# A running maximum in the softmax over nodes: the context of the first 20 tiles is made at the end of the layer ahead

## The chip, the cores and the metric

The kernel runs on one core of a Trainium2 chip. A core has a matrix engine (TensorE, PE in the profile; its weight loads are shown apart as PEld), a vector engine (VectorE, DVE), a scalar engine for activation functions (ScalarE, ACT), GpSimd (POOL), a queue engine (SyncE, SP) and 16 DMA engines. Each engine takes its own instructions in a fixed order, and waits on semaphores for the others. Data lies in on-chip memory of 128 partitions; PE writes to PSUM, a small memory of eight banks. The metric is the time of one execution on the device in microseconds (us), the median of several runs.

## The reference

The reference is a graph network on 3125 nodes of 256 features. Its first part adds a convolution over 100,000 edges to a mixer of four layers; after it come a gated mixture of experts, a second graph convolution with another mixer, and a routed mixture of experts. The change is in the four layers of the first mixer:

```python
def _linear_attn(x, Wq, Wk, Wv, Wo, bo):
    b, n, dm = x.shape
    split = lambda t: t.reshape(b, n, HEADS, DH).transpose(0, 2, 1, 3)
    scale = DH ** (-0.25)
    q = jax.nn.softmax(split(x @ Wq) * scale, axis=-1)
    k = jax.nn.softmax(split(x @ Wk) * scale, axis=-2)
    v = split(x @ Wv)
    context = jnp.einsum('bhnd,bhne->bhde', k, v)
    out = jnp.einsum('bhnd,bhde->bhne', q, context)
    out = out.transpose(0, 2, 1, 3).reshape(b, n, dm)
    return out @ Wo + bo

def _forward(x, ...):
    for i in range(DEPTH):
        h = _layernorm(x, ln1_g[i], ln1_b[i])
        x = x + _linear_attn(h, Wq[i], Wk[i], Wv[i], Wo[i], bo[i])
        h = _layernorm(x, ln2_g[i], ln2_b[i])
        x = x + (jax.nn.gelu(h @ W1[i] + b1[i], approximate=False) @ W2[i] + b2[i])
    return x
```

There are 8 heads of 32 columns. The softmax of `q` runs over the 32 columns of a head, that of `k` over all 3125 nodes: every column of `k` needs its maximum over the nodes before the first exponential, and the sum of the exponentials divides the context.

## The kernel before

**Tiles and groups.** The nodes lie in 25 tiles of 128 rows (the last has 53). Four tiles make a group; groups 0 to 5 have four tiles, group 6 only the last, short tile. `xs` holds the state, `H` the normalized rows with a column of ones, `K` and `Q` the keys and queries of all tiles, all in on-chip memory.

**One layer.** A layer starts when the keys and queries of all tiles are there. `kmax` (L960, L962) holds for each partition the maximum over the tiles so far. The layer transposes it (L987), reduces it over the partitions (L988) and brings it back as a row on all partitions by transposing a broadcast (L991). Then for each group DVE subtracts the maximum from `K` (L995), and ACT takes the exponential (L996); after these, ACT takes the exponentials of `Q` (L999). `shares(g)` (L1007 to L1009) divides the queries of a group by their sums. `context(b)` (two blocks of 128 columns) multiplies the exponentials of `K` with `H` over all 25 tiles (L1030) into one PSUM bank; the column of ones gives the sum. A float32 matmul of the program is two passes in the profile, so the 50 matmuls of a layer are 100 instances of L1030. The mean is scaled by the reciprocal sum (L1034, L1035), transposed (L1039), scaled and shifted (L1041), multiplied with the value weights (L1046), masked to heads (L1048), and multiplied with the output weights (L1051); `cw` (L1053) is what `attended(g)` multiplies the queries with (L1074), before it adds to `xs` (L1076).

**The rest of the layer** goes over the groups: for group g, the attention of group g+2, the norms of group g+2 and of group g-1, the MLP's hidden rows (`experts_hidden`, L284 and L287, Gelu on ACT) and its second half (`forward`, L1093, the bias row L839, the addition L1098). While group g is in its MLP, group g-1 already makes its keys and queries of the next layer (`keyed_queries`, L951 to L962). So at the end of a layer the MLP of the short group 6 runs, then the norm of group 5 (L194 and L195 for the statistics, L168 to L173 for a reciprocal root by Newton steps, L205, and on ACT L211, which writes `H`), its transposes (L230, L232), its key matmuls (L951), and those of group 6. In the first layer the keys come straight from the input, in a loop of its own.

**Work beside it.** Two generators are woven in between the matmuls: the building of the adjacency matrix (`g_` names, L718 to L731) and the sorting of the gating edges (`b_` names: matmuls L489, L491 and L506, DVE work L471 to L522, DMAs that fetch `kr` and `b_to`, and GpSimd's scatter L431). They are taken in turns counted per matmul group, not in time.

**Order.** The program's order is given by the generators and the calls to `next`, but a scheduler places the instructions on the engines, and so decides what stands ahead of what on each engine. Buffers are pools: the tag `mm` (two PSUM banks) serves the key matmuls, the hidden rows and the context; `hid` (eight buffers) serves the hidden rows, and at the start of a layer the means.

Of the kernel before, what the change touches and what calls it, by code (L numbers as in the profile page):

```python
# [8 lines left out]
F32 = mybir.dt.float32  # L9
BF16 = mybir.dt.bfloat16  # L10
I32 = mybir.dt.int32
AF = mybir.ActivationFunctionType
OP = mybir.AluOpType
AX = mybir.AxisListType
# [3 lines left out]
P = 128  # L18
N = 3125
D = 256  # L20
# [36 lines left out]
AT_FIRST = 0.4  # L57
OF_GATING = 1.28
LAG = 8
OF_SPLIT = 0.5  # L60
BETWEEN = 0.6
ALONE = 1.25
# [10 lines left out]
def rows_of(t):  # L73
    return P if t < NT - 1 else LAST


def tiles_of(g):
    return list(range(4 * g, min(4 * g + 4, NT)))
# [25 lines left out]
def tile_gps(ctx: ExitStack, tc: tile.TileContext, a, out):  # L104
# [691 lines left out]
    with ExitStack() as st:  # L796
# [120 lines left out]
        def begin(g):  # L917

            r, x, k = rows_of(tiles_of(g)[-1]), rows_in(K, g), len(tiles_of(g))
            rstd, nmr = ln_stats(x, r, twice=True)  # L920
            scaled(rows_in(H, g), x, r, rstd, nmr, k)
            scaled(rows_in(xs, g), x, r, rstd, nmr)
            store_rows(xn_d, xs[:, tiles_of(g)[0]:tiles_of(g)[-1] + 1, :], g)
# [10 lines left out]
        def turned(g, l, ln):  # L934
            nx = rows_in(H, g)
            hT = mp.tile([P, 2, 512], F32, name="hT", tag="hT", bufs=2)
            transposed(ps, hT, nx, rows_of(tiles_of(g)[-1]), [fcol(f"{ln}_g", 2 * l + c) for c in range(2)],
                       [fcol(f"{ln}_b", 2 * l + c) for c in range(2)])
            return hT

        def meanwhile(g):

            return min(1, len(tiles_of(g)) - 1)

        def keyed_queries(l, g, hT, j, wqkv, kmax):

            t = tiles_of(g)[j]
            r = rows_of(t)
            pqk = ps.tile([P, 512], F32, name="mm", tag="mm", bufs=2)
            for k in range(2):  # L950
                pace[0] = T.matmul(pqk[:r], lhsT=hT[:, k, j * P:j * P + r], rhs=wqkv[:, k, 0:512],  # L951
                                   start=(k == 0), stop=(k == 1))
            qmax = small.tile([P, 8], F32, name="qmax", tag="qmax")
            q3 = pqk[:r, 0:D].rearrange("p (h d) -> p h d", d=32)
            V.tensor_reduce(qmax[:r], q3, axis=AX.X, op=OP.max)
            V.tensor_tensor(Q[:r, t, :].rearrange("p (h d) -> p h d", d=32), q3,
                            qmax[:r, :, None].to_broadcast([r, 8, 32]), op=OP.subtract)
            S.activation(K[:r, t, :], pqk[:r, D:2 * D], AF.Copy)
            if t == 0:
                V.tensor_copy(kmax, pqk[:, D:2 * D])  # L960
            else:
                V.tensor_tensor(kmax[:r], kmax[:r], pqk[:r, D:2 * D], op=OP.max)  # L962

        def most():
            return mp.tile([P, D], F32, name="kmax", tag="kmax")

        wqkv, kmax = weights[0], most()
        begin(0)
        hT = turned(0, 0, "ln1")
        for g in range(NG):  # L970
            this = hT
            if g + 1 < NG:
                begin(g + 1)
            for j in range(len(tiles_of(g))):
                keyed_queries(0, g, this, j, wqkv, kmax)
                if g + 1 < NG and j == meanwhile(g):
                    hT = turned(g + 1, 0, "ln1")
                next(first, None)

        for l in range(LAYERS):  # L980
            last = l == LAYERS - 1
            wo, w1, w2 = weights[-3:]
            graph.summed()
            pt = ps.tile([P, 512], F32, name="tr", tag="tr", bufs=2)
            kmT = small.tile([P, 2], F32, name="kmT", tag="kmT")
            for c in range(2):
                T.transpose(pt[:, c * P:(c + 1) * P], kmax[:, c * P:(c + 1) * P], ident)  # L987
            V.tensor_reduce(kmT, pt[:, :D].rearrange("p (c n) -> p c n", c=2), axis=AX.X, op=OP.max)  # L988
            pb = ps.tile([P, 512], F32, name="tr", tag="tr", bufs=2)
            for c in range(2):  # L990
                T.transpose(pb[:, c * P:(c + 1) * P], kmT[:, c:c + 1].to_broadcast([P, P]), ident)  # L991
            some = [(tiles_of(g)[0], tiles_of(g)[-1] + 1, rows_of(tiles_of(g)[-1])) for g in range(NG)]
            for t0, t1, r in some:
                kg = K[:r, t0:t1, :]
                V.tensor_tensor(kg, kg, pb[:r, None, :D].to_broadcast([r, t1 - t0, D]), op=OP.subtract)  # L995
                S.activation(kg, kg, AF.Exp, scale=scale)  # L996
            for t0, t1, r in some:
                qg = Q[:r, t0:t1, :]
                tc.keep_in_program_order(S.activation(qg, qg, AF.Exp, scale=scale))  # L999
# [24 lines left out]

            def context(b):

                pc = ps.tile([P, 512], F32, name="mm", tag="mm", bufs=2)
                for t in range(NT):
                    r = rows_of(t)
                    T.matmul(pc[:, :D + 1], lhsT=K[:r, t, b * P:(b + 1) * P], rhs=H[:r, t, :],  # L1030
                             start=(t == 0), stop=(t == NT - 1))
                    if t % 6 == 5:
                        yield
                V.reciprocal(ksum[:, b:b + 1], pc[:, D:D + 1])  # L1034
                S.activation(mean[:, b, :], pc[:, :D], AF.Identity, scale=ksum[:, b:b + 1])  # L1035
                yield
                pt = ps.tile([P, 512], F32, name="tr", tag="tr", bufs=2)
                for c in range(2):
                    T.transpose(pt[:, c * P:(c + 1) * P], mean[:, b, c * P:(c + 1) * P], ident)  # L1039
                for c in range(2):  # L1040
                    S.activation(meanT[:, b, c, :], pt[:, c * P:(c + 1) * P], AF.Identity,  # L1041
                                 scale=fcol("ln1_g", 2 * l + c), bias=fcol("ln1_b", 2 * l + c))
                yield
                po = ps.tile([P, D], F32, name="o", tag="o", bufs=2)
                for c in range(2):
                    T.matmul(po[:, :P], lhsT=wqkv[:, c, 512 + b * P:512 + (b + 1) * P], rhs=meanT[:, b, c, :],  # L1046
                             start=(c == 0), stop=(c == 1))
                V.tensor_tensor(ctxT[:, b, :], po[:, :P], mask32, op=OP.mult)  # L1048
                yield
                po = ps.tile([P, D], F32, name="o", tag="o", bufs=2)  # L1050
                T.matmul(po, lhsT=ctxT[:, b, :], rhs=wo[:, b, :], start=True, stop=False)  # L1051
                add_row(po, l, P, 0, eighth)
                S.activation(cw[:, b, :], po, AF.Copy)  # L1053
                yield

            two = [context(0), context(1)]
            for _ in range(5):
                next(two[0])
            for _ in range(4):
                next(two[1])  # L1060
                next(two[0], None)
            next(two[1])
            qT = queries(0)
            for _ in two[1]:
                graph.summed()
# [39 lines left out]
            for g in range(NG):  # L1105
                n, k = cols_of(g), len(tiles_of(g))
                again = g - 1 if g and not last else None
                if g + 2 < NG:
                    attended(g + 2)
                normal(*([g + 2] if g + 2 < NG else []), *([] if again is None else [again]))  # L1110
                if g + 4 < NG:
                    shares(g + 4)
                hid = experts_hidden(ps, mp, w1, hT, n, 8, [fcol("mix_b1", 8 * l + i) for i in range(8)], bufs=8,
                                     between=hidden if k == 4 else None)
                before = None if again is None else turned(again, l + 1, "ln1")
                for j in range(max(k, 4 if before else 0)):
                    if j < k:
                        forward(g, hid, j)
                        if k == 4 or last:
                            beside(share)  # L1120
                            spread(0.5 * share)
                    if k < 4 and j == 0 and not last:
                        normal(g)
                    if g + 1 < NG and j == meanwhile(g):
                        hT = turned(g + 1, l, "ln2")
                    if before:
                        keyed_queries(l + 1, again, before, j, wqkv, kmax)
                        if k == 4:
                            beside(BETWEEN)
                            spread(BETWEEN)  # L1130
            if not last:
                before = turned(NG - 1, l + 1, "ln1")
                keyed_queries(l + 1, NG - 1, before, 0, wqkv, kmax)
                weights = [out_weights(l + 1), *hidden_weights(l + 1)]
        for _ in gating:
            buckets.scattered()
# [1100 lines left out]
```

## Time and profile before

| | |
|---|---|
| median of 3 runs | 3774.78 us (3763.15 to 3776.9) |
| the profiled execution: its time | 3769.39 us |
| its span | 3767.6 us |
| mean granted clock of PE in it | 0.959 |
| starts of the four layers, first L1030 | 93.0, 444.2, 853.9, 1243.2 us |
| first L1074 of the layers | 124.1, 475.7, 885.4, 1274.5 us |
| L1030, all layers | 400 passes, 103.9 us busy, 9.6 us idle ahead |
| L995 (DVE) and L996 (ACT), all layers | 28 each, 28.8 and 26.6 us busy |

The mixer takes about the first 1,600 us of the span. PE, DVE and ACT are named with the line of the kernel that issued the instruction; a row of the profile in order of time gives the start, the length, the engine, the line, the operation, what it writes and reads, the shape and the number of instructions put together, and in brackets the idle time before them with what ended it.

### The profile page before, as it was taken

How to read it: one execution, taken by the hardware profiler on the slowest of the kernel's cores; microseconds unless marked ns; L12 is line 12 of the kernel's file. 1: busy time of each engine (PE TensorE's matmuls, PEld its weight loads, DVE VectorE, ACT ScalarE, POOL GpSimd, SP SyncE). 2: the span in 40 equal slices, each digit the busy share in tenths (PEclk: the TensorE clock that was granted, in tenths of full speed). 3: DMA queues.
4: the chain of work that ended last, by engine and by line, in shares of the span. 5: the costliest groups of instructions: out<-in, count | busy, mean ns of one | idle time of the engine just before them, and what ended most of it. 6: DMA issues, size and time to landing. Idle time of an engine off the chain costs nothing. (4 is left out here: it accounts for less than half of the span.)

```text
span 3767.6 us, 50246 instructions
## 1 busy us (share of the span) xinstructions
PE 3492.3 (93%) x18153; PEld 2118.1 (56%) x18153; DVE 1903.1 (51%) x6827; ACT 1119.7 (30%) x2092; POOL 910.7 (24%) x915
## 2 busy tenths in 40 slices
PE   7999989988999988899899999998999999999998
PEld 3656666556666656544465565554444444444687
DVE  8757757676677766200418888762013032223421
ACT  5333342334332433200236675330013000000233
POOL 0044234532454154300002322200014010000233
PEclk9999999999999999999899999999999999999999
DMA  7013424651446166542476662003211222221576
GB/s 212 20 37 45 60 42 49 60 71 30 53 59 73 24 90 84 108 133 68 134 231 169 165 184 82 15 12 125 83 50 47 67 70 62 60 61 50 152 184 148
DMA packets 347700, 326.90 MB, mean 87 GB/s; under 512 B 144052, under 2 KB 311757, under 8 KB 346011
## 3 DMA queue, kind: packets, MB, share of 16 engines
q1 hardware_dynamic: 212763, 280.87, 28.2%
q10 hardware_dynamic: 105424, 26.40, 7.7%
q0 software_dynamic: 29232, 16.09, 2.7%
q8 instruction: 151, 2.47, 0.3%
q14 instruction: 130, 1.06, 0.1%
HBM read 239.75 MB, written 90.83 MB: 88 GB/s over the span
## 5 line engine op out<-in xcount | busy, mean ns | idle before, releaser
L431 POOL DMA_INDIRECT btab<-b_word,b_key x512 | 530.0, 1035 | 777.7 <-PE mm L284 408.2
L1190 PE MATMUL ag<-chb,xb 128*128 128x512 bf16 (+2 forms) x1950 | 404.1, 367 | 24.5 <-DMA chb<-A 16.6
L1190 PE MATMUL ag<-chb,Hb 128*128 128x512 bf16 (+1 forms) x1800 | 416.9, 385 | 3.9 <-issue 3.9
L284 PE MATMUL mm<-hT,w 128*128 128x512 f32 (+1 forms) x896 | 389.4, 571 | 8.0 <-DVE kmax L962 5.0
L1093 PE MATMUL o<-w,hid 128*128 128x256 f32 (+1 forms) x1600 | 388.7, 390 | 0.0
L1093 PEld LDWEIGHTS o<-w,hid 128*128 128x128 f32 (+1 forms) x1600 | 293.1, 191 | 51.1 <-issue 10.4
L1190 PEld LDWEIGHTS <-xb 128*128 128x128 bf16 (+1 forms) x2100 | 184.3, 98 | 243.4 <-issue 35.5
L1190 PEld LDWEIGHTS <-Hb 128*128 128x128 bf16 (+1 forms) x2100 | 183.9, 99 | 215.7 <-issue 22.0
L287 ACT ACTIVATE hid<-mm,fm 128x512 f32<-128x512 f32 (+1 forms) x336 | 210.7, 630 | 312.7 <-PE mm L284 281.4
L284 PEld LDWEIGHTS mm<-hT,w 128*128 128x128 f32 x896 | 162.1, 200 | 146.2 <-issue 128.1
L1392 PE MATMUL o<-f0w,hid 128*128 128x256 f32 (+1 forms) x800 | 216.3, 399 | 2.5 <-ACT hid L287 2.5
L951 PE MATMUL mm<-wqkv,hT 128*128 128x512 f32 (+1 forms) x400 | 207.3, 643 | 6.1 <-DVE kmax L962 3.4
L284 PE MATMUL mm<-xnT,f0w 128*128 128x512 f32 (+1 forms) x448 | 204.8, 582 | 5.3 <-DVEq L1656 4.1
L475 DVE SCALAR_TENSOR_TENSOR b_junk<-kr,b_key,b_tri 128x128 bf16<-128x128 f32 x512 | 175.1, 342 | 27.3 <-DMA kr<-keys_g 24.0
L1783 POOL DMA_INDIRECT slots<-rb,r_ati x50 | 49.4, 987 | 501.3 <-DVE rb L1776 395.7
L731 ACT ACTIVATE g_st<-gc 128x400 bf16<-128x400 f32 x192 | 94.2, 500 | 255.4 <-PE gc L727 177.3
L1392 PEld LDWEIGHTS o<-f0w,hid 128*128 128x128 f32 (+1 forms) x800 | 141.5, 191 | 39.5 <-issue 14.7
L718 DVE TENSOR_TENSOR g_ol<-g_all,g_lo 128x1024 bf16<-128x1024 bf16 (+1 forms) x199 | 136.1, 684 | 40.9 <-PE gc L727 27.3
L2119 DVE TENSOR_TENSOR a2T<-a2T,ag 128x512 f32<-128x512 f32 x24 | 15.9, 688 | 277.4 <-PE ag L1190 277.3
L727 PEld LDWEIGHTS <-g_ol 128*128 128x128 bf16 (+1 forms) x1589 | 120.0, 165 | 61.4 <-issue 46.8
L232 ACT ACTIVATE hT<-tr,fm 128x512 f32<-128x512 f32 (+1 forms) x126 | 86.5, 719 | 164.1 <-PE tr L230 158.2
L1910 POOL DMA_INDIRECT out_dram<-yo,dest x56 | 87.5, 1562 | 189.8 <-DVE yo L1909 101.8
(504 smaller groups left out, 5697.5 us busy)
## 6 DMA issues: line engine op xcount, KB each, us to landing
hot<-low_d SPq DMA_DIRECT2D x125, 384.0 KB
kr<-keys_g SPq DMA_DIRECT2D x256, 128.0 KB
f1w<-in_f_w_dram SPq DMA_DIRECT2D x56, 512.0 KB
slots<-blank SPq DMA_DIRECT2D x14, 1950.0 KB
A<-g_st ACTq DMA_DIRECT2D x24, 800.0 KB
chb<-A SPq DMA_DIRECT2D x48, 397.2 KB
chb<-A SPq DMA_DIRECT2D x48, 384.0 KB
chb<-A SPq DMA_DIRECT2D x120, 128.0 KB
```

Of the source, the lines that this page charges most:

```text
L284: pace[0] = T.matmul(ph[:, :n], lhsT=w1[:, k, hb * P:(hb + 1) * P], rhs=xT[:, k, :n], start=(k == 0), stop=(k == 1))
L287: S.activation(h[:, :n], ph[:, :n], AF.Gelu, bias=bias[hb])
L431: d = G.indirect_dma_start(out=btab.rearrange("(n o) -> n o", o=1), out_offset=bass.IndirectOffsetOnAxis(ap=self.key[:, c:c + 1].bitcast(I ...
L475: ranked = V.scalar_tensor_tensor(junk, kr[:, (j % EACH) * P:(j % EACH + 1) * P], self.key[:, c0 + j:c0 + j + 1], self.tri, op0=OP.is_equa ...
L718: V.tensor_tensor(lo[:r, :, :k], self.all[:r, :, :k], self.lo[:r, None, c:c + k].to_broadcast([r, P, k]), op=OP.is_equal)
L727: T.matmul(p[:, j, :], lhsT=lo[:r, :, j], rhs=hi[:r, j, :h], start=True, stop=True)
L731: S.activation(stage.rearrange("p h (l j) -> p h l j", l=2)[:, :, :, j0:j0 + k], p.rearrange("p j (l h) -> p h l j", l=2), AF.Copy)
L951: pace[0] = T.matmul(pqk[:r], lhsT=hT[:, k, j * P:j * P + r], rhs=wqkv[:, k, 0:512], start=(k == 0), stop=(k == 1))
L1093: pace[0] = T.matmul(po[:r], lhsT=hid[hb][:, j * P:j * P + r], rhs=w2[:, hb, :], start=(hb == 0), stop=False)
L1190: T.matmul(acc[fb, g][:, :n], lhsT=Xb[:r, s, i, fb * P:(fb + 1) * P], rhs=ch[:r, at:at + n], start=first, stop=last, skip_group_check=g == ...
L1392: T.matmul(po[:r], lhsT=hid[hb][:, j * P:j * P + r], rhs=w2[:, hb, :], start=(hb == 0), stop=False)
L1910: d = G.indirect_dma_start(out=out, out_offset=bass.IndirectOffsetOnAxis(ap=dest[:, c:c + 1], axis=0), in_=yo[:, c, :], in_offset=None, bo ...
```

## The change

The maximum is taken twice. The first time, `kmax` holds the first 20 tiles (groups 0 to 4, `GA = 5`): from it a first maximum `top` is made, groups 0 to 4 are subtracted and exponentiated, and the two blocks of context over these 20 tiles are made and copied out of PSUM, with their sums. This is a generator, `early`, whose steps stand between the key matmuls of group 5 and around those of group 6, at the end of the layer ahead (for the first layer, at the end of the loop that makes its keys). The second time, at the start of the layer, `kmax` holds all tiles: groups 5 and 6 are subtracted by the final maximum and exponentiated, and their context (5 tiles) is made. A factor `less`, the exponential of the difference of the two maxima, scales the first part and its sum before they are added. The transposed maximum has a PSUM bank of its own (`kb`). The number of matmuls of the context is the same; new are, for each layer, a second set of maximum transposes, and the copies, sums and products that join the parts.

```diff
+GA = 5
...
+        def peaks(kmax):
+            p = ps.tile([P, 2, D], F32, name="kb", tag="kb", bufs=1)
+            kmT = small.tile([P, 2], F32, name="kmT", tag="kmT")
+            for c in range(2):
+                T.transpose(p[:, 0, c * P:(c + 1) * P], kmax[:, c * P:(c + 1) * P], ident)
+            V.tensor_reduce(kmT, p[:, 0].rearrange("p (c n) -> p c n", c=2), axis=AX.X, op=OP.max)
+            for c in range(2):
+                T.transpose(p[:, 1, c * P:(c + 1) * P], kmT[:, c:c + 1].to_broadcast([P, P]), ident)
+            return kmT, p[:, 1]
+
+        def below_peak(g, pb):
+            t0, t1, r = some[g]
+            kg = K[:r, t0:t1, :]
+            V.tensor_tensor(kg, kg, pb[:r, None, :].to_broadcast([r, t1 - t0, D]), op=OP.subtract)
+            S.activation(kg, kg, AF.Exp, scale=scale)
+
+        def weighted(b, t0, t1):
+            pc = ps.tile([P, 512], F32, name="mm", tag="mm", bufs=2)
+            for t in range(t0, t1):
+                r = rows_of(t)
+                T.matmul(pc[:, :D + 1], lhsT=K[:r, t, b * P:(b + 1) * P], rhs=H[:r, t, :],
+                         start=(t == t0), stop=(t == t1 - 1))
+            return pc
+
+        def early(kmax):
+            part["top"], pb = peaks(kmax)
+            for g in range(GA):
+                below_peak(g, pb)
+                yield
+            part["mean"] = mp.tile([P, 2, D], F32, name="part", tag="hid", bufs=8)
+            part["sum"] = small.tile([P, 2], F32, name="psum", tag="psum", bufs=1)
+            for b in range(2):
+                pc = weighted(b, 0, 4 * GA)
+                V.tensor_copy(part["sum"][:, b:b + 1], pc[:, D:D + 1])
+                S.activation(part["mean"][:, b, :], pc[:, :D], AF.Copy)
+                yield
...
         for g in range(NG):
...
+            if g == GA:
+                ahead = early(kmax)
+                next(ahead)
             for j in range(len(tiles_of(g))):
                 keyed_queries(0, g, this, j, wqkv, kmax)
+                if g == GA:
+                    next(ahead)
...
+            if g >= GA:
+                next(ahead)

         for l in range(LAYERS):
...
-            for t0, t1, r in some:
-                kg = K[:r, t0:t1, :]
-                V.tensor_tensor(kg, kg, pb[:r, None, :D].to_broadcast([r, t1 - t0, D]), op=OP.subtract)
-                S.activation(kg, kg, AF.Exp, scale=scale)
+            top, pb = peaks(kmax)
+            for g in range(GA, NG):
+                below_peak(g, pb)
+            less = small.tile([P, 2], F32, name="less", tag="less", bufs=1)
+            V.tensor_tensor(less, part["top"], top, op=OP.subtract)
+            S.activation(less, less, AF.Exp, scale=scale)
...
             def context(b):
-                for t in range(NT):
...
-                V.reciprocal(ksum[:, b:b + 1], pc[:, D:D + 1])
-                S.activation(mean[:, b, :], pc[:, :D], AF.Identity, scale=ksum[:, b:b + 1])
+                pc = weighted(b, 4 * GA, NT)
+                V.scalar_tensor_tensor(ksum[:, b:b + 1], part["sum"][:, b:b + 1], less[:, b:b + 1], pc[:, D:D + 1],
+                                       op0=OP.mult, op1=OP.add)
+                V.reciprocal(ksum[:, b:b + 1], ksum[:, b:b + 1])
+                V.scalar_tensor_tensor(mean[:, b, :], part["mean"][:, b, :], less[:, b:b + 1], pc[:, :D],
+                                       op0=OP.mult, op1=OP.add)
+                S.activation(mean[:, b, :], mean[:, b, :], AF.Identity, scale=ksum[:, b:b + 1])
...
             two = [context(0), context(1)]
-            for _ in range(5):
+            for _ in range(4):
                 next(two[0])
-            for _ in range(4):
                 next(two[1])
-                next(two[0], None)
-            next(two[1])
...
                 before = None if again is None else turned(again, l + 1, "ln1")
+                if before and g == NG - 1:
+                    ahead = early(kmax)
+                    next(ahead)
                 for j in range(max(k, 4 if before else 0)):
                     if j < k:
                         forward(g, hid, j)
...
                     if before:
                         keyed_queries(l + 1, again, before, j, wqkv, kmax)
+                        if g == NG - 1:
+                            next(ahead)
...
             if not last:
+                next(ahead)
                 before = turned(NG - 1, l + 1, "ln1")
                 keyed_queries(l + 1, NG - 1, before, 0, wqkv, kmax)
+                next(ahead)
```

More of the change, by code (lines that the diff above doesn't have):

```diff
@@ L965, in most @@
             return mp.tile([P, D], F32, name="kmax", tag="kmax")
+        some = [(tiles_of(g)[0], tiles_of(g)[-1] + 1, rows_of(tiles_of(g)[-1])) for g in range(NG)]
+        def peaks(kmax):
[19 more added lines that the diff above has]
+            return pc
+        part = {}
+        def early(kmax):
[10 more added lines that the diff above has]
+                yield
         wqkv, kmax = weights[0], most()
@@ L983, in tile_gps @@
             graph.summed()
[L984 to L992, printed above, removed]
-            for t0, t1, r in some:
-                kg = K[:r, t0:t1, :]
-                V.tensor_tensor(kg, kg, pb[:r, None, :D].to_broadcast([r, t1 - t0, D]), op=OP.subtract)
-                S.activation(kg, kg, AF.Exp, scale=scale)
+            top, pb = peaks(kmax)
[4 more added lines that the diff above has]
+            S.activation(less, less, AF.Exp, scale=scale)
             for t0, t1, r in some:
@@ L1025, in context @@
             def context(b):
-                pc = ps.tile([P, 512], F32, name="mm", tag="mm", bufs=2)
-                for t in range(NT):
[L1029 to L1033, printed above, removed]
-                V.reciprocal(ksum[:, b:b + 1], pc[:, D:D + 1])
-                S.activation(mean[:, b, :], pc[:, :D], AF.Identity, scale=ksum[:, b:b + 1])
+                pc = weighted(b, 4 * GA, NT)
[5 more added lines that the diff above has]
+                S.activation(mean[:, b, :], mean[:, b, :], AF.Identity, scale=ksum[:, b:b + 1])
                 yield
```

## The prediction

> **What bounds the kernel now.** I read the page first, then the instructions of TensorE (PE) in order of time around the four starts of a layer, then those of VectorE (DVE) and ScalarE (ACT) in the same stretches, and last the busy time and the clock in 5 us stretches.
>
> ```profile
> PE 3492.3 (93%) x18153; PEld 2118.1 (56%) x18153; DVE 1903.1 (51%) x6827; ACT 1119.7 (30%) x2092; POOL 910.7 (24%) x915
> ```
>
> PE sets the pace, so an edit here is worth what it does to PE's idle time, and to PE's clock. The lines for the start of layer 1 on PE, ACT and DVE (start, length, engine, line; in brackets the idle time before and what ended it):
>
> ```profile
> 423.45 0.29 PE L839 MATMUL o<-rows,ones 3*53 3x256 bf16 x1
> 423.67 0.44 PE L230 MATMUL tr<-ident,H 128*128 128x128 f32 x2
> 426.88 3.70 PE L951 MATMUL mm<-wqkv,hT 128*128 128x512 f32 x8
> 435.66 1.92 PE L951 MATMUL mm<-wqkv,hT 128*53 128x512 f32 x4
> 444.19 17.01 PE L1030 MATMUL mm<-H,K 128*128 128x257 f32 x62 [2.40 <-ACT K L996]
> 475.70 0.70 PE L1074 MATMUL o<-cw,qT 128*128 128x256 f32 x2
> 421.90 2.06 ACT L211 ACTIVATE H<-xs,ln_nmr,rs_y 128x256 f32<-128x256 f32 x4
> 419.75 0.16 DVE L205 SCALAR_TENSOR_TENSOR ln_nmr<-ln_mv,rs_y 128x4 f32<-128x4 f32 x1
> 423.78 0.41 DVE L1098 TENSOR_TENSOR xs<-xs,o 53x256 f32<-53x256 f32 x1 [3.87 <-PE o L839]
> ```
>
> To be seen: the layer's tail is tight. Group 5's norm (L205) is done at 419.75, ACT writes H at 421.90, and PE goes from the last MLP row (L839) straight into group 5's transposes. The weak place is after the last key tile (end 437.6): 6.6 us to the context (L1030), in which PE works about 2. Starts 2 and 3 show two more things:
>
> ```profile
> 850.82 0.66 PE L991 MATMUL tr<-ident,kmT 128*128 128x128 f32 x2 [4.97 <-DVE kmT L988]
> 849.87 0.47 DVE L483 TENSOR_SCALAR b_to<-b_to,b_own 25x1024 bf16<-25x1024 bf16 x1 [4.94 <-DMA b_to<-his_g]
> 1223.93 5.86 PE L951 MATMUL mm<-wqkv,hT 128*128 128x512 f32 x8 [0.16 <-ACT hT L232]
> 1240.80 7.20 DVE L995 TENSOR_TENSOR K<-K,tr 128x1024 f32<-128x1024 f32 x7
> 1242.05 7.08 ACT L996 ACTIVATE K<-K 128x1024 f32<-128x1024 f32 x7 [2.11 <-DVE K L995]
> 1225.00:1230.00 5.00, 5.00 (x11) 1.88 (x9) 2.36 (x9) 0.98 (x2) 0.00 (x0) 0.67 0.02 6
> 1250.00:1255.00 5.00, 5.00 (x25) 4.35 (x24) 4.89 (x6) 5.00 (x7) 0.00 (x0) 1.00 0.00 0
> ```
>
> At start 2 a DMA for the edge sort delays DVE, and through DVE the maximum. In the two stretch rows (busy time of PE, weight load, DVE, ACT, POOL, each with its count) the last number but two is the granted clock: after a gap PE runs slow, and eight passes of L951 take 5.86 us instead of 3.70.
>
> **What the change does, step by step.** Its instruction order was read from the built program. S is the start of group 5's key matmuls (L951), T0 the end of the early context, A the first L1074. From the PE rows, before: S = 426.88, 826.58, 1223.93 and A = 475.70, 885.35, 1274.50 for layers 1 to 3.
>
> *1. Group 5's norm gets late.* On DVE the five subtractions of the early groups now stand between the links of group 5's reciprocal-root chain (L171 to L173), ahead of its L205; on ACT the table load and the five exponentials stand ahead of its four L211. PE must transpose H next, with only eight tiny matmuls (0.56) to do meanwhile. A subtraction is 1.15 (7.20 for six and a small one), an exponential 1.06, the table load 1.28. Layer 1: the two pairs of peak transposes are inside group 6's hidden matmuls, so the first subtraction can start near 421.8. Five make 5.8; the DVE work among them and L1098, which waits for the MLP row till about 424.9, make 2.3. The fifth ends at 429.9, its exponential at 431.0, the transposes start about 431.5, not 423.67: +7.9. Layer 2 alike: 830.7, not 824.10, +6.6. Layer 3, where the hidden matmuls run slow and DVE idles 7.93 before its L1098: two subtractions are in before it, but a scan, a mask and a pick now precede L205; 1227.1, not 1220.58: +6.5. Together +21.0; the second pair of peak transposes (0.44 a pair) is in these. Bounds: 0 (DVE's idle time before L1098, 3.87, 3.02 and 7.93, takes all of it) to 9 each (all five subtractions, five exponentials less their overlap, and the load in line).
>
> *2. Clock after that gap.* The gap is about 6 us; by the pair 5.86 and 3.70 the next eight passes lose 2.2. Layer 3 loses this already. +4.4 for layers 1 and 2; bounds 0 and 7.
>
> *3. From S to A.* The key tiles of group 5 take 7.7 (two eights of 3.70 and gaps), small matmuls 1.1, the 80 early passes of L1030 80 x 0.215 = 17.2 (from 3.50 less overlap for 14, in the fast stretch), the last key tile 1.9: T0 = S + 27.9. The final maximum is then known long before T0, so PE no longer waits for L962. After T0: copy of the sum, an unrelated 0.6, peak transposes, reduce, transposes: first late subtraction at T0+1.9; its exponential ends at T0+4.2; the first late matmul comes at T0+4.3, as today 2.4 after PE ran dry, so this wait stays. Twenty passes at a mostly half clock: T0+12.1. DVE has two sums, reciprocals and products of queries queued ahead (2.35 + 0.55 + 2.29 = 5.2) and ends them at T0+11.9. Then the added work: two sums with scale (0.17 each, as L1034), two 128x256 sums with scale (0.52, from the row L1704), two reciprocals: T0+13.4. ACT's scaling, transposes and meanT reach T0+15.3; ctxT stands behind two more query sums (2.35), T0+16.3; L1051, its row and cw: A = T0+18. So S to A is 45.9, against 48.8, 58.8 and 50.6. Layer 1: -2.9. Layer 2: -12.9, as the DMA wait is no longer ahead of the maximum, +2 for two edge-sort rounds that now stand before the late context: -10.9. Layer 3, with its slow passes on both sides: -2.5. Together -16.3. The copies of the early context (ACT 0.38 each, as L1053) and of its sums (DVE 0.17) lie under the 80 passes; without that cover they cost 0.8 a layer. The tiny exponential of the scale was taken at 0.2 (between 0 and 0.31, the smallest ACT row near). T0 to A has bounds 14 (no queueing on DVE) and 21.
>
> *4. Layer 0.* No MLP precedes; five subtractions (5.8) come into DVE's key work, whose maxima free the matmul banks. PE waits about 3 and loses 2.5 by the clock; the saving after is 1.8: +3.7; bounds -4 and 8.
>
> *5. PE in the new chain.* From T0+12 to A it has about 3 us of work; formerly passes of L1030 covered block 0's chain. A second clock loss, taken as 1.5 at each of four starts: +6; bounds 0 and 3.5 each.
>
> *6. Query shares.* Today all seven groups' shares are done under the context; now groups 4 to 6 come after A, partly in front of the norm of group 0, while its four H no longer wait for the other group's four: +0.5 each, +2; bounds -2 and 6 each.
>
> Sum: 21.0 + 4.4 - 16.3 + 3.7 + 6 + 2 = **+20.8 us**. DMAs are the same; SP and POOL get no new instruction, and their loads move with the work around.
>
> On terms 2 and 5 the Trainium skill says, in "TensorE: Matmul & The Clock Gate" (Part 1: The HAM clock gate; HAM oscillation), that an idle window of some 3.4 us halves the clock and some 3.4 us of work restore it. It speaks against a change that opens a gap. By it a gap loses 1.7 us, and terms 2 and 5 would be 3.4 and 6.8; the rows show longer slow spells (two stretches at 0.50 after 1204), so the rows were used.
>
> **Which time.** The profiled execution had a span of 3767.6 and a time of 3769.39; with the sum, 3790. The median of the three runs is 5.4 higher, 3774.78, and what is measured later is such a median: 3774.8 + 20.8 = 3796 (its own range 3783 to 3808).
>
> **Rivals.**
> - *Half as late.* DVE takes most subtractions in its idle time before L1098 (3.87 to 7.93, for it), and the new chain costs no clock. Term 1 falls by half (-10.5), term 5 goes (-6): +4, 3779. Against it: the order on DVE, which puts links of the chain behind subtractions.
> - *Faster.* The layer's end hides everything: terms 1 and 2 vanish (-25.4), and T0 to A is 14, with queues not in the way (4 x -4 = -16): 20.8 - 41.4 = -20.6, 3754. For it: starts wait 2.4 to 12.5 for maximum and exponentials. It decides if H of group 5 is not late by over 1 us.
> - *Shares in the way.* DVE's displaced shares (2.5 a group, four groups, 10 a layer) delay the norms of the first groups, six of the ten unhidden at each start: +24 on top, 3820. For it: after A, PE already waits for norms (L211). Against it: DVE idles 7.76 soon after.
> - *It changes nothing*, as the scheduler leaves the early work late: excluded by the order, where 40 of 50 context matmuls a layer stand by the last key tile.
>
> **How the numbers follow.** Forecast 0.50, half as late 0.25, faster 0.12, shares in the way 0.13. About 0.5% (19 us) is what a measurement of this kernel tells from no change. Slower by more: 0.42 of the forecast's 0.50 and 0.13: 0.55; within: 0.33; faster by more: 0.12. The range leaves out the far side of faster and of shares: 3760 to 3822.
>
> **What would show it.** Right: the transposes of group 5's H 6 to 8 us behind the MLP row, ended by ACT's H; a wait of about 2.4 still ahead of the late context; PE at half clock near A; no wait at start 2 for the sort's DMA. Wrong: these transposes follow the MLP row at once, or S to A is under 42 us.

## The result and the profile after

The changed kernel is slower by 0.7%. Its median is 3806.31 us (3797.23 to 3811.43, 6 runs), that of the kernel before on the same chip 3777.78 us (3763.15 to 3785.32, 6 runs); the ratio is 1.0071, with a 95% interval of 1.0052 to 1.0089. The profiled execution took 3805.28 us, with a span of 3803.6 (before: 3767.6) and a mean granted clock of 0.954 (before: 0.959). On another chip the ratio came out at 1.0086 (1.0060 to 1.0111). Medians of the same kernel differ by up to 1% between chips (before: 3744 to 3784), so only ratios are compared below, each with runs of before on its own chip.

The start of layer 1 on PE, in order of time (start, length, engine, line, operation; in brackets the idle time before and what ended it). Lines of the changed kernel have moved by one to forty: L231 are the transposes, L952 the key matmuls, L992 the context, L1114 the attention, L212 ACT's writing of `H`.

```profile
431.69 0.41 PE L840 MATMUL o<-rows,ones 3*53 3x256 bf16 x1
438.32 2.17 PE L231 MATMUL tr<-ident,H 128*128 128x128 f32 x8 [5.73 <-ACT H L212]
442.38 5.57 PE L952 MATMUL mm<-wqkv,hT 128*128 128x512 f32 x8
452.57 8.93 PE L992 MATMUL mm<-H,K 128*128 128x257 f32 x40
473.43 0.43 PE L978 MATMUL kb<-ident,kmT 128*128 128x128 f32 x2 [0.70 <-DVE kmT L976]
476.33 6.84 PE L992 MATMUL mm<-H,K 128*128 128x257 f32 x20 [2.46 <-ACT K L985]
488.48 1.98 PE L1114 MATMUL o<-cw,qT 128*128 128x256 f32 x8
501.85 2.16 PE L231 MATMUL tr<-ident,H 128*128 128x128 f32 x8 [3.79 <-ACT H L212]
```

Three places stand out. Between the last MLP row (431.69) and group 5's transposes (438.32) there are now 6.6 us, where before there were 0.2; the eight key passes behind them are slow. After the early context PE still waits 2.46 for the last exponentials, and the 20 late passes take 6.84 us, where 40 early ones took 8.93; this place is no new cost, as before waited 2.40 at its one start of the context, and its first 62 passes took 17.01. And after the first L1114, group 0's transposes come 13.4 us later, where it was 10.5 (475.70 to this row of before):

```profile
486.18 2.17 PE L230 MATMUL tr<-ident,H 128*128 128x128 f32 x8 [2.53 <-ACT H L211]
```

The first place on DVE, in the changed kernel and layer 1:

```profile
423.27 0.42 DVE L976 TENSOR_REDUCE kmT<-kb 128x2 f32<-128x256 f32 x1 [3.58 <-PE kb L975]
427.35 1.22 DVE L984 TENSOR_TENSOR K<-K,kb 128x1024 f32<-128x1024 f32 x1 [2.91 <-PE kb L978]
432.54 1.21 DVE L984 TENSOR_TENSOR K<-K,kb 128x1024 f32<-128x1024 f32 x1
434.15 1.21 DVE L984 TENSOR_TENSOR K<-K,kb 128x1024 f32<-128x1024 f32 x1
435.44 1.18 DVE L984 TENSOR_TENSOR K<-K,kb 128x1024 f32<-128x1024 f32 x1
436.98 0.14 DVE L206 SCALAR_TENSOR_TENSOR ln_nmr<-ln_mv,rs_y 128x4 f32<-128x4 f32 x1
```

The chain of group 5's norm ends in L206, which was at 419.75, 3.7 us ahead of the MLP row, and is now at 436.98, 5.3 behind it. The early work delays it in two ways. Five subtractions of 1.2 us (four are shown) stand between its links; and the reduction and the first subtraction each wait for PE's transposes (3.58 and 2.91), which stand among the MLP matmuls, while the chain waits behind them, though it needs neither.

The third place, on DVE after the first L1114:

```profile
494.43 1.18 DVE L1052 TENSOR_REDUCE qsum<-Q 128x32 f32<-128x1024 f32 x1
499.51 1.22 DVE L1054 TENSOR_TENSOR Q<-Q,qsum 128x1024 f32<-128x1024 f32 x1
501.05 0.10 DVE L206 SCALAR_TENSOR_TENSOR ln_nmr<-ln_mv,rs_y 128x4 f32<-128x4 f32 x1
```

Sums and products of the query shares of groups 2 and 3 stand between the links of group 0's norm. Before, all shares were done under the 100 context passes. The list of PE's waits (total, times, longest) adds up the first and the third place; the first row is of before:

```profile
PE tr L230 <- ACT H L211: 26.3, 7, 13.8
PE tr L231 <- ACT H L212: 46.3, 9, 13.9
```

The longest wait, 13.8 and 13.9, stands at the start of the program in both kernels; what is left of it grew from 12.5 to 32.4 us.

### The profile page after: what moved, and what is told of

The parts are those of the page before. It is cut to its first block, busy times and chain, and to the rows that moved or that the text cites. A ratio compares the mean times of both kernels' runs of the same rounds, so it can differ in the third digit from the quotient of the medians.

```text
span 3803.6 us, 50209 instructions
## 1 busy us (share of the span) xinstructions
PE 3507.7 (92%) x18077; PEld 2125.8 (56%) x18169; DVE 1902.9 (50%) x6859; ACT 1122.1 (30%) x2104; POOL 911.0 (24%) x915
## 5 line engine op out<-in xcount | busy, mean ns | idle before, releaser
L285 PE MATMUL mm<-hT,w 128*128 128x512 f32 (+1 forms) x896 | 395.8, 580 | 12.6 <-DVE kmax L963 6.6
L952 PE MATMUL mm<-wqkv,hT 128*128 128x512 f32 (+1 forms) x400 | 211.0, 653 | 9.2 <-DVE kmax L963 6.3
L1439 PEld LDWEIGHTS o<-f0w,hid 128*128 128x128 f32 (+1 forms) x800 | 142.3, 192 | 40.6 <-issue 14.1
```

The source lines that it names most:

```text
L285: pace[0] = T.matmul(ph[:, :n], lhsT=w1[:, k, hb * P:(hb + 1) * P], rhs=xT[:, k, :n], start=(k == 0), stop=(k == 1))
L1439: T.matmul(po[:r], lhsT=hid[hb][:, j * P:j * P + r], rhs=w2[:, hb, :], start=(hb == 0), stop=False)
```

## The experiments

Each kernel was timed in five rounds against the kernel before. "Queued behind" means an order on one engine without a wait for completion: `tc.issue_after(i)` puts what its block issues on `i`'s engine behind `i`.

| kernel | median us | before, same chip | ratio and 95% interval |
|---|---|---|---|
| changed, first chip | 3806.31 | 3777.78 | 1.0071 (1.0052 to 1.0089) |
| changed, again | 3780.69 | 3750.31 | 1.0086 (1.0060 to 1.0111) |
| e1 norm first | 3759.87 | 3744.47 | 1.0040 (1.0025 to 1.0056) |
| e2 shares behind | 3753.46 | 3744.47 | 1.0025 (1.0014 to 1.0035) |
| e3 both | 3745.28 | 3744.47 | 0.9995 (0.9980 to 1.0009) |
| e4 all at the start | 3784.27 | 3744.47 | 1.0116 (1.0096 to 1.0135) |
| e5 maximum under the context | 3736.69 | 3750.31 | 0.9962 (0.9944 to 0.9980) |
| e7 subtractions spread | 3738.47 | 3750.31 | 0.9971 (0.9954 to 0.9989) |
| e8 idle passes | 3759.84 | 3750.31 | 1.0028 (1.0008 to 1.0048) |
| e9 two shares early | 3745.53 | 3783.59 | 0.9903 (0.9883 to 0.9923) |
| e10 five shares early | 3755.88 | 3783.59 | 0.9925 (0.9906 to 0.9944) |
| e11 at the start, shares behind | 3814.95 | 3783.59 | 1.0083 (1.0065 to 1.0101) |

**e1: group 5's norm first.** `nmr_of[0]` is the last instruction of the norm written last (L206).

```diff
                 if before and g == NG - 1:
-                    ahead = early(kmax)
-                    next(ahead)
+                    ahead, behind = early(kmax), nmr_of[0].ins
+                    with tc.issue_after(behind):
+                        next(ahead)
...
                         if g == NG - 1:
-                            next(ahead)
+                            with tc.issue_after(behind):
+                                next(ahead)
```

> VectorE's part of the early work (reduction of the maximum, five subtractions) is queued behind the last instruction of group 5's norm at the starts of layers 1 to 3; nothing else is moved. Theory (group 5's norm is late because the early work stands in front of it): the transposes of group 5's H follow the MLP row within about 0.5 us, where the changed kernel has gaps of 6.6, 6.8 and 7.4 us between their starts; three gaps of together 17.9 us go, and up to 8 us of slow clock behind them: 18 to 26 us off 3806, 3780 to 3788, ratio to before 1.001 to 1.003. Rival 1 (the joining work after the last key tile costs the time): less than 5 us off, ratio 1.006 or more. Rival 2 (the gap only moves: the early exponentials, now later, hold up the early context): the transposes come on time, but S to T0 grows by about what the gap gave, ratio 1.005 to 1.008.

The gaps went, as expected: the transposes of group 5's H now start within 1.5 us of the MLP row (428.34, row 429.14, in layer 1). The ratio fell from 1.0071 to 1.0040, some 12 us (17 us from the second measurement, 1.0086), less than the 18 to 26 expected. The rest shows on PE, a few us later:

```profile
428.34 0.44 PE L233 MATMUL tr<-ident,H 128*128 128x128 f32 x2
429.14 0.29 PE L842 MATMUL o<-rows,ones 3*53 3x256 bf16 x1
431.42 3.70 PE L954 MATMUL mm<-wqkv,hT 128*128 128x512 f32 x8 [0.76 <-ACT hT L235]
438.12 5.20 PE L954 MATMUL mm<-wqkv,hT 128*128 128x512 f32 x8 [2.99 <-DVE rs_y L174]
```

The first eight key passes are fast again (in layer 3 they take 5.73, as they were slow there before the change too), but the next eight wait 2.99 us. The subtractions stand now in front of the reductions that free the key tiles' two PSUM banks; layers 2 and 3 have 2.46 and 1.00 there. So a good part of the gain is real, and a part of it moved, as rival 2 said, to another place than it named: no exponential was late.

**e2: the shares behind the norm.**

```diff
                 normal(g)
-                shares(g + 2)
+                with tc.issue_after(nmr_of[0].ins):
+                    shares(g + 2)
...
                 if g + 4 < NG:
-                    shares(g + 4)
+                    with tc.issue_after(nmr_of[0].ins):
+                        shares(g + 4)
```

> The shares of groups 2 to 6 are queued on VectorE behind the last instruction of the norm that the kernel writes ahead of them; the early work stays as in the changed kernel. Theory (displaced shares delay the norm of group 0 after A): A to the transposes of group 0's H goes from 14.1, 13.4, 13.4 and 12.6 us to about 10.5 at each of four starts, 8 to 15 us off, ratio to before 1.003 to 1.005. Rival (the shares have to be done anyway and only hold up the next group's Q): H of group 0 comes earlier, but PE waits as long later, less than 4 us off, ratio 1.006 to 1.008.

From A to the transposes of group 0's H it takes 9.8, 10.5, 9.6 and 11.9 us in place of 14.1, 13.4, 13.4 and 12.6: 11.7 us. In layer 1, from A:

```profile
473.95 1.98 PE L1116 MATMUL o<-cw,qT 128*128 128x256 f32 x8
484.44 1.92 PE L233 MATMUL tr<-ident,H 128*128 128x128 f32 x8 [0.82 <-ACT H L214]
```

The ratio is 1.0025, some 17 us below the first measurement of the changed kernel, a little more than expected. Most of it lies ahead of group 0's transposes: from A to the first hidden matmul of group 6 the four layers take 7.9, 1.7, 6.2 and -2.1 us less than in e1 on the same chip, together 13.7, of which 11.2 stand before these transposes.

**e3: both.**

> Both orders together. If the late norm and the displaced shares are two separate losses: 26 to 40 us off, 3766 to 3780, ratio to before 0.997 to 1.001. If the joining work is the main loss: 1.005 or more.

The ratio is 0.9995, no difference from before. The two losses are separate: e1 took off 0.0031, e2 0.0046, both together 0.0076, within what the intervals allow. What is left of the change neither gains nor loses.

**e4: the joined sum without the move.** Second maximum, sums with scale and both parts of the context, all at the start of the layer (`early` runs there to its end, then the second maximum).

```diff
+            ahead = early(kmax)
+            for _ in range(GA + 2):
+                next(ahead)
             top, pb = peaks(kmax)
...
-            if g == GA:
-                ahead = early(kmax)
-                next(ahead)
...
-                if before and g == NG - 1:
-                    ahead = early(kmax)
-                    next(ahead)
...
-                        if g == NG - 1:
-                            next(ahead)
...
-                next(ahead)
                 before = turned(NG - 1, l + 1, "ln1")
                 keyed_queries(l + 1, NG - 1, before, 0, wqkv, kmax)
-                next(ahead)
```

> The same two-part sum with its scale, but nothing is moved ahead: both maxima (the first one now of all groups), all subtractions and both parts of the context stand at the start of the layer. Theory: the edit's added work alone costs 2 to 5 us at each of four starts (second maximum with four transposes, sums with scale, scaling after both blocks): 8 to 20 us above before, ratio 1.002 to 1.005, and group 5's H is on time. Rival (the added work on the chain is what costs): ratio 1.007 or more.

My theory missed this: 1.0116, 43 us above before, not 8 to 20. Layer 1 of this kernel on PE shows the price of the joined form:

```profile
458.38 20.40 PE L992 MATMUL mm<-H,K 128*128 128x257 f32 x80 [2.40 <-ACT K L985]
483.35 8.43 PE L992 MATMUL mm<-H,K 128*128 128x257 f32 x20 [2.57 <-ACT K L985]
497.29 0.70 PE L1110 MATMUL o<-cw,qT 128*128 128x256 f32 x2
511.40 2.16 PE L231 MATMUL tr<-ident,H 128*128 128x128 f32 x8 [5.62 <-ACT H L212]
```

There are two waits for exponentials where there was one, and behind the second PE is slow: 8.43 us for the 20 late passes, at a granted clock of 0.59; in e11's layer 2 the same 20 took 5.20 at 1.00. Also, block 0's chain of transposes and products no longer lies under block 1's passes, and the shares come after A. So the two-part sum is itself costly in this form, and the move ahead gives a part of that back.

**e11: the same, with the shares behind the norm** (the edit of e2 on e4).

> The run with everything at the start of the layer, with the shares of groups 2 to 6 queued behind the norm as before. Theory (its loss has two parts: a second maximum with its wait and slow clock, and shares in front of the norm of group 0): A to the transposes of group 0's H goes from 14.0, 14.1, 12.3 and 14.3 us to about 10.5, 8 to 15 us off, ratio to before 1.0075 to 1.0095. Rival (the shares cost nothing there): 1.011 or more.

As expected: 1.0083, and 9.6 us from A to the transposes at all four starts. Of e4's loss, a quarter to a third was the shares. The rest belongs to the two-part sum itself; how it divides into the second maximum, its wait, the slow clock and the chain of block 0, the runs don't show.

**e8: idle passes in the gap of the changed kernel.**

```diff
                         forward(g, hid, j)
+                        if before and g == NG - 1:
+                            for _ in range(20):
+                                T.transpose(part["kb"][:, 0, 0:P], ident, ident)
```

> The changed kernel with 20 idle transposes of 128x128 on PE, whose output nothing reads, between the MLP row and the transposes of group 5's H, where PE waits 5.2 to 6.1 us: the norm stays as late, PE stays warm. Theory (the wait is the loss, the clock behind it a small part): the first eight key passes take about 3.7 us instead of 5.6 to 6.1, 4 to 8 us off the changed kernel, ratio to before 1.005 to 1.006. Rival (the half clock is the larger part): 12 us or more off, ratio 1.004 or less; if it does nothing, 1.007.

The ratio is 1.0028, but this doesn't tell wait from clock: with the added transposes the scheduler also changed DVE's order, and in layer 1 put one subtraction in front of group 5's L206 instead of five. The transposes there come 2.2 us after the MLP row, not 6.6, and the added transposes fill this time, so no wait is left. The run is 21 us faster than the changed kernel on the same chip. It agrees with e1 on the cause of the gap, the subtractions ahead of the norm, and says nothing on the share of the clock.

**e5: the final maximum under the context** (on e3). The second block's early passes are written behind the final maximum.

```diff
                 keyed_queries(l + 1, NG - 1, before, 0, wqkv, kmax)
-                next(ahead)
...
-            if g >= GA:
+            if g == GA:
                 next(ahead)
...
             S.activation(less, less, AF.Exp, scale=scale)
+            next(ahead)
```

> On top of both orders: the early passes of the second block (40 on PE) are written behind the final maximum, so that they lie between it and the late passes. Theory (after the last key tile PE waits for maximum and exponentials, then runs slow, as in the changed kernel): in the run with both orders PE waits 0.66 and 2.46 us there and the 20 late passes take 6.83 us instead of 4.3; with passes to do meanwhile 3.1 + 2.5 us go at each of four starts, some 1 us is lost to the wait for the first reduction: 14 to 22 us off, ratio to before 0.994 to 0.996. Rival (the sums of the query shares on VectorE, 5.2 us ahead of the joining, set A anyway): at most 2 us at each start, ratio 0.997 to 1.000.

0.9962: faster than before, between what the theory and the rival expected. The start of e5's layer 1 on PE:

```profile
443.32 2.42 PE L994 MATMUL mm<-H,K 128*128 128x257 f32 x10
445.58 0.38 PE L977 MATMUL kb<-ident,kmax 128*128 128x128 f32 x2
446.89 10.75 PE L994 MATMUL mm<-H,K 128*128 128x257 f32 x46
460.50 0.69 PE L1085 MATMUL tr<-ident,mean 128*128 128x128 f32 x2 [2.67 <-ACT mean L1081]
```

Maximum, subtractions and exponentials now lie under PE's passes: early and late ones make one run of 46 without a wait, at full clock. But the next wait took a part of the gain, as the rival said: PE waits 2.67 for the scaled mean, because two sums, reciprocals and products of queries stand ahead of the joining on DVE. And the clock behind the wait was worth less than the 2.5 us counted for it: the 20 late passes take 5.20 at full clock (layer 2), not 4.3, against 6.83.

**e7: subtractions spread over the key tiles** (on e5): each of the later ones is queued behind the maximum of a key tile, `kmax_of[0]`, in place of `behind`.

> As the run before it, and subtractions two to five each stand behind the maximum of a key tile of group 5 instead of together ahead of them. Theory (in front of the key tiles they hold up the reductions that free the key tiles' banks: with both orders PE waits 2.99 us after eight key passes and the next eight take 5.26 us, not 3.70): 3 to 4.5 us off at each of three starts, 9 to 13 us below the run before it, ratio to before 0.990 to 0.993. Rival (one subtraction more for each key tile makes VectorE the pace, 2.5 us a tile against 1.9 on PE): within 4 us of the run before it.

0.9971, the same as e5; the rival holds, though the run doesn't show whether VectorE's pace per tile is the reason. In layer 1 the wait falls from 2.99 to 1.00, but from S to A layers 2 and 3 take 52.0 and 50.4 us, against 47.6 and 45.7 in e5, so nothing is gained this way.

**e9 and e10: the shares early** (on e5). In `early`, behind the subtractions:

```diff
+            for t0, t1, r in some[:GA]:
+                qg = Q[:r, t0:t1, :]
+                tc.keep_in_program_order(S.activation(qg, qg, AF.Exp, scale=scale))
+            with tc.issue_after(kmax_of[0].ins):
+                for g in range(2):
+                    shares(g)
...
-            for t0, t1, r in some:
+            for t0, t1, r in some[GA:]:
                 qg = Q[:r, t0:t1, :]
...
-            shares(0)
-            shares(1)
```

> On top of the maximum under the context: the exponentials of the queries of groups 0 to 4, and the shares of groups 0 and 1, are written behind group 5's last key tile, ahead of the early context, so that they lie under its 80 passes. Theory (in the run with the maximum under the context, two sums, reciprocals and products of queries, 5.2 us on VectorE, stand ahead of the joining; PE waits 2.67 us for the scaled mean and runs at half clock until A): 3 to 5 us off at each of four starts, ratio to before 0.991 to 0.994. Rival (in front of the last key tile's maximum they delay the final maximum instead): no gain, ratio 0.996 to 0.999.

> As the run before it, with the shares of groups 0 to 4 all there. Theory (VectorE idles under the early passes, 7.7 and 4.1 us in the first layer's trace, and nothing waits for it there): 0 to 8 us below the run before it, ratio 0.990 to 0.994. Rival (13 us of shares in front of the last maximum are more than that idle time): 4 us or more above the run before it.

e9 is the fastest of all: 0.9903, 38 us below before on its chip. Its layer 1 on PE:

```profile
443.47 10.75 PE L996 MATMUL mm<-H,K 128*128 128x257 f32 x46
454.15 0.44 PE L1091 MATMUL tr<-ident,mean 128*128 128x128 f32 x2
459.38 0.70 PE L1123 MATMUL o<-cw,qT 128*128 128x256 f32 x2
```

No wait is left from the early passes to A. From S to A it takes 43.9, 46.7 and 42.5 us, where before had 48.8, 58.8 and 50.6. e10 (all five groups there) is 10 us slower than e9, as its rival said, and the trace shows how: DVE's copy of the early sum stands behind thirteen instructions of shares, so its PSUM bank is free late, and PE waits.

```profile
446.26 4.12 PE L996 MATMUL mm<-H,K 128*128 128x257 f32 x10 [2.16 <-ACT part L1029]
```

**The changed kernel again**, on the chip of e5, e7 and e8.

> The changed kernel once more, on the chip of the three runs above. If the chip does not matter to the ratio: 1.005 to 1.009.

1.0086, and the same gaps from the MLP row to group 5's transposes: 6.5, 6.8 and 7.4 us (first chip 6.6, 6.8, 7.4).

## Why the prediction was right, and where it was not

The forecast was 3796 us, slower; measured were 3806. The sum was +20.8 and the profiled spans differ by +36.0, the medians by +28.5. S, T0 and A are those of the prediction. Steps 2, 3 and 5 overlap in the trace: the slow key passes and three of the four clock losses lie between S and A. Its terms:

1. *Group 5's norm late: right in cause, 3 us too large.* The step from row to transposes grew by 6.4, 6.1 and 5.4 us, together 17.9; predicted 21.0. e1 removes it. In layer 1 two of the five subtractions ran ahead of the row, so that the fifth ended 4.9 us behind it, where the working had 6.5. The working also left out that the reduction waits for PE, with the norm behind it (3.58); the last exponential ends as ACT begins with H, as predicted.
2. *Clock after the gap: right for the key passes.* The first eight take 5.57, 6.00 and 6.08 us, against 3.70, 3.70 and 5.86: +4.4, as predicted. The granted clock in layer 1 is the last number but two of the row below. By the window of some 3.4 us that the page "TensorE: Matmul & The Clock Gate" of the Trainium skill (Part 1) states, a gap would lose an estimated 1.7 us; the two stretches that were fast before lost 1.9 and 2.3. No step had the transposes ahead of these passes, 2.17 us for eight where before had 1.09 (layer 2): from their start to S it takes 4.06, 4.06 and 4.43 us, against 3.21, 2.48 and 3.35, together +3.5, some of it waits for the edge sort.

```profile
440.00:445.00 5.00, 4.32 (x22) 2.30 (x22) 2.10 (x7) 1.93 (x3) 0.00 (x0) 0.50 0.03 10
```

3. *S to A: gain 2.7 us too large.* The interval changed by -2.7, -4.1 and -2.4, together -9.2; without the 4.4 of slow key passes, which step 2 has, -4.6, -6.4 and -2.6, together -13.6, against -16.3. Layer 3 came out as predicted and layer 1 gained 1.7 more; layer 2 failed, at the words "the DMA wait is no longer ahead of the maximum". The wait is no longer there, but it is not gone. It stands ahead of the joining:

```profile
893.40 0.47 DVE L484 TENSOR_SCALAR b_to<-b_to,b_own 25x1024 bf16<-25x1024 bf16 x1 [4.98 <-DMA b_to<-his_g]
893.80 2.33 DVE L1052 TENSOR_REDUCE qsum<-Q 128x32 f32<-128x1024 f32 x2
898.74 0.20 DVE L1073 SCALAR_TENSOR_TENSOR ksum<-psum,less,mm 128x1 f32<-128x1 f32 x1
```

   DVE waits 4.98 for the edge sort's DMA, then makes the shares, then joins, while PE waits 3.74 for the mean. The edge sort also keeps PE itself waiting ahead of the late passes (2.22, 1.19 and 0.68), more than the 2 that were allowed for it. T0 to A is 24.4 there, against 20 predicted; elsewhere it is 16 to 18, against 18. The wait of about 2.4 ahead of the late context stayed in the other layers (2.57, 2.46 and 2.46), as said. These sizes are of one trace: in the second execution, on another chip, S to A is 48.6, 56.4 and 48.4 us, where the first has 46.1, 54.7 and 48.2.
4. *Layer 0: wrong in sign.* A comes 3.5 us earlier, of which 2.9 lie before any changed work; the rest is -0.6, where +3.7 was predicted.
5. *Clock in the new chain: mostly not there.* From 480 on, with the end of the late passes and the chain to A, the granted clock in layer 1 is 0.97 and 1.00 (5 us each); only in layer 2 the chain has 0.82. The clock loss sits in the late passes themselves (6.8 to 8.4 us for 20), and step 3 had counted it. It need not set A: in layer 1 of the second execution these passes ran at full clock (5.20 us), and PE then waited for the scaled mean, from T0 to A 17.7 us in all. The working's 0.215 us for a pass fits the early ones (40 in 8.93), not the late ones (20 in 5.20).

```profile
469.26 5.20 PE L992 MATMUL mm<-H,K 128*128 128x257 f32 x20 [2.46 <-ACT K L985]
476.80 1.01 PE L1082 MATMUL tr<-ident,mean 128*128 128x128 f32 x4 [1.84 <-ACT mean L1078]
```

6. *Query shares: mis-sized, the largest error.* "+0.5 each" was taken; from A to group 0's transposes it is +3.9, +2.9, +3.0 and +1.8, together 11.5, and e2 shows some 17 us for the shares in all (1.0071 to 1.0025; from e1 to e3, on one chip, 1.0040 to 0.9995). The step weighed the shares against DVE's idle time, and not against the chain that they stand in. The rival *shares in the way*, at 0.13, had the mechanism and, with 24 us, nearly the size.

So the mechanism of the late norm was right, and that the total came so close was in part luck, as errors of both signs met: 9.5 to 15 missing in step 6, 2.7 in step 3 and the 3.5 ahead of S, against 3, 4 and 6 too much in steps 1, 4 and 5. This leaves 2 to 8 missing; the medians say 7.7 (28.5 less 20.8), the two profiled spans 15.2, of which 6.1 are a spell of half clock told of at the end. Of the four signs of being right that the prediction named, two came: the transposes 6.6 to 7.4 us behind the row, and the wait of 2.4 ahead of the late context, in three layers. Two did not: near A the clock is mostly full, and at start 2 the sort's DMA is still waited for.

The rival *faster* is refuted for this order; e9 shows that the same idea, with another order, gives a gain. The clock goes along with this only in part. Added up over 100 us stretches of the first 1,700 us (twice what is missing to a clock of 1), PE ran at half clock for about 182 us before, 214 and 204 in two executions of the changed kernel, 148 in e3 and 130 in e9 (other chips); but e1, which is slower than before, has 160, and e5, which is slower than e9, has 116. What stays open is how much of each gap is wait and how much clock: e8 was to tell it and didn't.

## What to carry to other kernels

Work that is moved ahead into idle time stands in an engine's queue in front of something: look for the chain of short dependent instructions whose gaps a scheduler will fill, and put the moved work behind the end of that chain. A reduction split in two needs its second wait covered by work that does not depend on it, here the other block's early passes; without this the split cost about what the move gave (e11, with no move, 1.0083; e3, with it, 0.9995). What the long stage used to hide (here the query shares) has to find a new cover, and that is costed like an edit of its own.

## What was not expected of the hardware

The same stretch of the same kernel ran mostly at half clock in one execution and at full clock in another: from group 6's first hidden matmul to its MLP row, ahead of layer 1, the changed kernel took 15.1 us in one execution (granted clock 0.58) and 9.1 in the other, on another chip (1.00), with small matmuls and waits of 0.3 and 0.4 us in it both times. A difference of 6 us in one stretch of one trace is therefore no price of an edit by itself; it was taken as one only where other layers, or the ratios, showed it too.
